# Moving the adjacency's combinations into the first graph's attention of a two-layer graph network

## The chip, the core and the metric

The kernel runs on one core of a Trainium2 chip. The metric is the device time of one execution in microseconds (us), from the first to the last instruction. Five engines run at the same time, each through its own list of instructions in order, and meet only through semaphores: PE (matrix products and transposes), DVE (elementwise work and reductions), ACT (activations and copies), POOL (elementwise work, and it issues DMA transfers) and SP (it only issues DMA transfers). An instruction that has to wait holds up everything behind it on its engine.

## The reference, cut to what matters

There are B = 16 graphs of N = 1024 nodes with C = 256 features, all with the same adjacency matrix.

```
# layer 0, for each graph
h  = relu(layernorm(x))
A_s = 2 * | |sigmoid(mean_j - mean_i) - 0.5| - 0.5 |      # weights of pairs of nodes
g  = relu((h^T @ (adj * A_s)) * para)                     # para: 256 x 1024
q  = g^T; k, v = h @ kv_w
x  = x + softmax(q k^T * scale) v                         # 4 heads of 64
# layer 1
h  = relu(layernorm(x))
An = adj + I
deg = columnsums(An) + rowsums(An) - diagonal(An)
A_hat = An * rsqrt(deg)[:, None] * rsqrt(deg)[None, :]
x  = x + batchnorm(relu(batchnorm((A_hat @ h) @ W1^T + b1)) @ W2^T + b2)
```

The batch norms are taken over all graphs. Two things in layer 1 are independent of the graph and are made once: the degrees, and sums and differences of blocks of `An` for a block matrix product with seven instead of eight products (the "combinations").

## The kernel before, in words

**The main loop.** `attention()` walks over the units of all graphs: a graph has four units (pair of heads x half of the query nodes), a unit four steps. A step issues scores (PE, 128x1024 to PSUM, L841), their exponentials (ACT, L849), the running sum of the exponentials (DVE, L868 and L871), and the product with the values for the step before (PE, L882). At a unit's end `sums()` makes the row sums (PE, L899), copies them to a tile `row` (ACT, L901), and POOL sends them through DRAM (`sums_d<-row`, L902, then `inv<-sums_d`, L907). Two steps later `add_output()` uses `inv` on DVE.

**The background.** Beside the attention of graph b, `background(b)` yields pieces of other work, each with an estimated cost; `attention()` takes pieces until a due amount is reached in each step (`advance`). `weave(main, (start, side), ...)` walks through `main` and takes one piece of each side from `main`'s piece number `start` on. `soon(action)` puts an action behind the next piece. The order in which the code emits instructions is the order on each engine: nothing is rearranged later.

Beside graph b stand the keys, values and queries of graph b + 1 (`keys_values`, `queries`), its weights (`weigh`: rows of the adjacency, Abs and Tanh on ACT, L401 and L409, a product with the row on DVE, L388), and layer 1's first product and hidden layer for graph b - 1 (`aggregate`, `hidden`). Graphs 0 and 1 get their queries by `plain_queries`, sixteen pieces that PE works through two per step; graphs from 2 on by `queries`, with seven products. The last of these is `seventh`: it adds the product and by `soon` lets `finish(1, 0)` follow, which multiplies a block of q by `para` on DVE (L449). Then come the values: four pieces of a matmul `pv` (PE) and two copies out of PSUM (DVE, L591), in one of two PSUM banks in turn.

**The degrees** (`degrees()`) run beside graph 0, woven in from its first pieces on: for each of eight 128-row tiles of the transposed adjacency a load (SP, L204), a copy with accumulated sum (ACT, L220), and two small operations for the diagonal (DVE, L222, L223); at the end a reciprocal root on POOL (`rsqrt`, L81 and L82). `columns_of(dinv)` then spreads the result on DVE (`cb_deg`, L188), and PE transposes it to `cbp_deg` (L199), from where ACT copies it to `dbc` (L200).

**The combinations** (`graph()`) run beside graph 1 in eight pieces, two per 256-row pair of blocks. A piece loads 128x1024 twice by SP (`au_f`, L239), adds the identity where the diagonal lies (POOL, L246), makes four differences (POOL, L251 to L254), and stores seven blocks to DRAM by three transfers from POOL (`aht_d`, L256 to L258). `aggregate` reads `aht_d` later, beside graph 1 for the first time.

**Buffers.** The pieces' `au_f` tiles, the rows of `weigh` and the tiles of `degrees` share the three buffers "adj". The pieces' `two` and `one`, the tiles `row`, `cb_deg`, `cb_c` and `y` share the four buffers "y", handed out in turn: who takes one waits until its last user, four takings before, is done. `w1` (weights of the hidden layer) and `dbc` have a place each, first needed beside graph 1.

Of the kernel before, what the change touches and what calls it, by code (L numbers as in the profile page):

```python
# [10 lines left out]
F32 = mybir.dt.float32  # L11
# [6 lines left out]
P = 128  # L18
# [5 lines left out]
def gnn_two_layers_kernel(  # L24
# [12 lines left out]
    nc = tc.nc  # L37
# [8 lines left out]
    TH = 2  # L46
# [37 lines left out]
    def layers(shifted):  # L84
# [30 lines left out]
        def soon(action):  # L115

            queue.append(action)
# [87 lines left out]
            return tile_  # L205

        deg_sm = big.tile([P, 6, NT], F32, name="deg")
        w1 = big.tile([P, CC, H1], F32, name="w1")
        dbc = const.tile([P, N], F32, tag="dbc", name=f"dbc_{kind}")
        row, diag, col, deg, tmp_deg, dinv = (deg_sm[:, i, :] for i in range(6))  # L210

        def degrees():

            nc.sync.dma_start(out=w1, in_=w1_t.rearrange("(k p) j -> p k j", p=P))
            nc.vector.tensor_reduce(row, rows.rearrange("p q t -> p t q"), AX.X, ALU.add)
            for t in range(NT):
                a = load_adj_t(t, "at")
                yield 0.0
                blk = a[:, t * P : (t + 1) * P]
                nc.scalar.activation(a, a, AF.Copy, accum_out=col[:, t : t + 1])  # L220
                db = p1.tile([P, P], F32, tag="s1", name=f"db_{t}")
                nc.vector.tensor_mul(db, blk, ident)  # L222
                nc.vector.tensor_reduce(diag[:, t : t + 1], db, AX.X, ALU.add)  # L223
                yield 0.0
            nc.vector.tensor_add(deg, col, row)
            nc.vector.tensor_sub(deg, deg, diag)
            rsqrt(dinv, deg, 1.0, tmp_deg)

        def graph():


            HT, HB = NT // 2, FB // 2
            for t in range(HT):
                for part in range(2):
                    cols = slice(part * HB, (part + 1) * HB)
                    a = p3.tile([P, 2, NH, HB], F32, tag="adj", name=f"au_{kind}_{t}_{part}")
                    for n in range(2):
                        r = slice((t + n * HT) * P, (t + n * HT + 1) * P)
                        nc.sync.dma_start(  # L239
                            out=a[:, n], in_=adj_t[r].rearrange("p (m c) -> p m c", m=NH)[:, :, cols]  # L240
                        )
                    yield 0.0
                    for n in range(2):
                        if part == t * P // HB:
                            blk = a[:, n, n, t * P % HB : t * P % HB + P]
                            nc.gpsimd.tensor_add(blk, blk, ident)  # L246
                    two = py.tile([P, 2, HB], F32, tag="y", name=f"two_{t}_{part}")
                    one = py.tile([P, HB], F32, tag="y", name=f"one_{t}_{part}")
                    b12, b21, b22 = a[:, 0, 1], a[:, 1, 0], a[:, 1, 1]
                    sub = nc.gpsimd.tensor_sub  # L250
                    sub(two[:, 0], b12, a[:, 0, 0])  # L251
                    sub(two[:, 1], b22, two[:, 0])
                    sub(b12, b22, b12)
                    sub(one, b21, two[:, 1])  # L254
                    dst = aht_d[:, t // TH, :, t % TH, cols].rearrange("i p c -> p i c")
                    nc.gpsimd.dma_start(out=dst[:, :4], in_=a.rearrange("p n m c -> p (n m) c"))  # L256
                    nc.gpsimd.dma_start(out=dst[:, 4:6], in_=two)
                    nc.gpsimd.dma_start(out=dst[:, 6], in_=one)  # L258
                    yield 0.0

        class Norm:

# [166 lines left out]
        def queries(b):  # L429
# [65 lines left out]

            def seventh(m):
                add(c21, m, c21)
                soon(lambda: finish(1, 0))

            for i, (left, right, midway, after) in enumerate(  # L500
                (
# [94 lines left out]
        def aggregate(b):  # L596


            pieces = []
            order = (0, 2, 5, 1, 4, 6, 3)  # L600

            def load(upto):
                while len(pieces) <= min(upto, 7 * NP // 2 - 1):
                    i, th = divmod(len(pieces), NP // 2)
                    i = order[i]
                    a = p8.tile([P, TH, FB], F32, tag="w", name=f"aht_{b}_{i}_{th}")
                    nc.sync.dma_start(out=a, in_=aht_d[i, th])
                    pieces.append(a)

            load(4)  # L610
            yield 0.0
            a11, a12, a21, a22 = quarters("b", b)
            at = ats[b] = [
                p3.tile([P, CC, FB], F32, tag="ht", name=f"at_{b}_{g}") for g in range(NH)
            ]
            c11, c12, c21, c22 = (at[g][:, c, :] for c in (0, 1) for g in (0, 1))
            add, sub = nc.vector.tensor_add, nc.vector.tensor_sub

            def scale(c, g):
                nc.vector.tensor_mul(c, c, dbc[:, g * FB : (g + 1) * FB])  # L620

            def first(m):
                nc.scalar.copy(c12, m)
                sub(a11, s1s["b", b], a11)

            def second(m):
                add(c11, m, c12)
                sub(a12, a12, a11)
                soon(lambda: scale(c11, 0))

            def fifth(m):
                add(c22, m, c21)
                add(c12, m, c12)
                soon(lambda: scale(c22, 1))

            def sixth(m):
                add(c21, m, c21)
                soon(lambda: scale(c21, 0))

            def seventh(m):  # L640
                add(c12, m, c12)
                scale(c12, 1)

            for i, (left, after) in enumerate(
                (
                    (a11, first),
                    (a12, second),
                    (a11, lambda m: add(c12, m, c12)),
                    (a21, lambda m: add(c21, m, c12)),
                    (None, fifth),  # L650
                    (a22, sixth),
                    (a12, seventh),
                )
            ):
                made = bank(f"pa_{b}_{i}")
                left = left or s1s["b", b]
                for th in range(NP // 2):
                    n = i * NP // 2 + th
                    load(n + 5)
                    for j in range(TH):  # L660
                        t = th * TH + j
                        product(
                            made, left[:, t, :], pieces[n][:, j, :], t == 0, t == NT // 2 - 1
                        )
                    if th == NP // 2 - 1:
                        after(made)
                    elif i == 0:
                        combine("b", b, nc.vector)
                    yield 1.71

        def hidden(b):
# [7 lines left out]
            for n, (g, j) in enumerate(parts):  # L679
                i = b * NH + g  # L680
                made = bank(f"py_{i}_{j}")
                for k in range(CC):
                    product(
                        made, w1[:, k, j * P : (j + 1) * P], at[g][:, k, :], k == 0, k == CC - 1
                    )
                y = py.tile([P, FB], F32, tag="y", name=f"y_{i}_{j}")
                nc.scalar.activation(y, made, AF.Identity, bias=b1[:, j : j + 1])  # L687
# [47 lines left out]
        def background(b):  # L735

            if b == 0:
# [8 lines left out]
                w, products = weighers[1], keys_values(1)  # L746
# [12 lines left out]
                broadcast_row(dbc, cbs, "deg")  # L759
                yield 1.0  # L760
                yield from prepare(2, products)
                return
# [1 line left out]
            gather = aggregate(b - 1)  # L764
            if b + 1 < B:
                w, products, norm = weighers[b + 1], keys_values(b + 1), normed(b - 1)
                combined = graph() if b == 1 else iter(())
                yield from weave(islice(products, 4), (0, islice(w, 4)), (0, islice(combined, 4)))
                yield from weave(
                    queries(b + 1), (0, double(w)), (0, combined), (9, islice(norm, 5))  # L770
                )
                yield next(gather)
                yield from weave(products, (0, norm))
            else:
# [218 lines left out]
        with st:  # L993
            if shifted:
                for b in range(B):
# [6 lines left out]
                    run(islice(weighers[b], AHEAD))  # L1002
                    run(weave(plain_queries(b), (0, weighers[b])))
                    if b == 0:
                        run(degrees())
                        broadcast_row(dbc, columns_of(dinv, "deg"), "deg")
# [5 lines left out]
                    if b == 0:  # L1012
                        run(graph())
# [355 lines left out]
```

## Time and profile before

| | before |
|---|---|
| time, median of 3 runs | 2678.98 us (2678.57 to 2681.39) |
| span of the profiled execution | 2678.6 us |
| mean granted PE clock | 0.986 |
| busy DVE | 1744.0 us |
| busy ACT | 1336.8 us |
| busy POOL | 552.8 us |
| DMA, mean over the span | 133 GB/s |
| one 128x1024 operation: p<-sc on ACT, acc<-acc,p on DVE | 1019 ns, 1224 ns |
| one 64x512 matmul, pg<-w,h_a | 594 ns (they overlap: 24 take 5.32 us) |

How to read it: busy time on its engine is a line's mean duration times its count. What decides is which engine never rests, and for the stretches where it does, what ended its pause. In the timeline a pause stands in brackets at a row's end, with the operation that ended it: `[0.79 <-DVE v L591]`. A row of the waits has the waiting operation, what it waited for, and then the sum in us, the number of times and the longest. A row of a table by stretch has the stretch, its length in us, then the busy us (and instructions) of PE, of PE's weight loads, of DVE, ACT and POOL, then the granted clock, the share of the DMA engines and GB/s.

### The profile page before, as it was taken

What the parts mean: (1) busy time and instruction counts of PE and PEld (TensorE: products, weight loads), DVE (VectorE), ACT (ScalarE), POOL (GpSimd) and SP (SyncE); (2) the same over time, 40 slices, a digit from 0 to 9 for tenths busy, and PEclk for the clock granted to TensorE, in tenths of its full rate; (3) what the DMA queues carried; (4) which work ended last, traced back from release to release, by engine and by line L of the source; (5) the groups of instructions that cost most, each with busy time, mean ns of one, the idle gap of its engine ahead of it and who ended that gap; (6) DMA issues with size and microseconds to landing.
All of it is one profiled execution on the core that took longest, in us unless ns stands there. A gap on an engine that the chain in (4) does not pass through costs nothing. (4 is left out here: it accounts for less than half of the span.)

```text
span 2678.6 us, 32187 instructions
## 1 busy us (share of the span) xinstructions
PE 2577.6 (96%) x11882; PEld 953.2 (36%) x11882; DVE 1744.0 (65%) x2768; ACT 1336.8 (50%) x1937; POOL 552.8 (21%) x632
## 2 busy tenths in 40 slices
PE   8897899999999999999999999999999999999994
PEld 3232333333333333333333333333333333334443
DVE  5556576666767575766667676757676675557674
ACT  5652363735455454636364544545463633335544
POOL 1016111111111111111111111111112111126653
PEclk9999899999999999999999999999999999999997
DMA  4325524242333414242524233242424233455559
GB/s 165 105 66 182 183 83 170 79 152 88 130 103 95 134 61 172 79 169 83 170 79 142 91 124 113 75 152 66 169 83 169 79 117 104 133 198 199 193 181 369
DMA packets 134759, 355.60 MB, mean 133 GB/s; under 512 B 17984, under 2 KB 38976, under 8 KB 128448
## 3 DMA queue, kind: packets, MB, share of 16 engines
q1 hardware_dynamic: 109120, 278.44, 30.3%
q0 software_dynamic: 25472, 75.00, 8.4%
q8 instruction: 96, 1.57, 0.2%
q14 instruction: 71, 0.58, 0.1%
HBM read 278.67 MB, written 74.71 MB: 132 GB/s over the span
## 5 line engine op out<-in xcount | busy, mean ns | idle before, releaser
L849 ACT ACTIVATE p<-sc 128x1024 f32<-128x1024 f32 x512 | 495.3, 1019 | 615.8 <-PE sc L841 615.1
L871 DVE TENSOR_TENSOR acc<-acc,p 128x1024 f32<-128x1024 f32 x384 | 470.1, 1224 | 143.6 <-ACT p L849 123.3
L841 PE MATMUL sc<-q,k 64*128 64x512 f32 x2048 | 512.7, 619 | 11.3 <-ACT p L849 11.3
L882 PE MATMUL o<-p,v 128*64 128x512 f32 x2048 | 496.4, 605 | 0.0
L158 PE MATMUL pg<-w,h_a 128*64 128x512 f32 x1600 | 359.7, 594 | 10.1 <-DVE w L388 4.9
L158 PE MATMUL pa<-aht,h_b 128*64 128x512 f32 x1536 | 343.5, 592 | 0.0
L841 PEld LDWEIGHTS sc<-q,k 64*128 64x128 f32 x2048 | 177.1, 187 | 333.8 <-issue 291.7
L902 POOL DMA_DIRECT2D sums_d<-row x64 | 37.6, 588 | 1053.8 <-ACT row L901 1053.8
L158 PE MATMUL py<-at,w 128*64 128x512 f32 x1024 | 230.4, 592 | 0.0
L388 DVE SCALAR_TENSOR_TENSOR w<-w,adj 128x1024 f32<-128x1024 f32 x128 | 157.1, 1227 | 108.2 <-ACT w L409 97.3
L882 PEld LDWEIGHTS o<-p,v 128*64 128x64 f32 x2048 | 124.4, 136 | 285.8 <-issue 283.7
L158 PEld LDWEIGHTS pg<-w,h_a 128*64 128x64 f32 x1600 | 115.4, 137 | 239.5 <-issue 211.3
L158 PEld LDWEIGHTS pa<-aht,h_b 128*64 128x64 f32 x1536 | 110.3, 137 | 213.3 <-issue 198.1
L687 ACT ACTIVATE y<-py,vec 128x512 f32<-128x512 f32 x128 | 87.6, 684 | 168.4 <-PE py L158 111.4
L401 ACT ACTIVATE w<-cbc,csum 128x512 f32<-128x512 f32 x256 | 170.0, 715 | 0.0
L868 DVE TENSOR_TENSOR acc<-p,p 128x1024 f32<-128x1024 f32 x64 | 78.9, 1233 | 109.3 <-ACT p L849 109.3
L158 PE MATMUL pv<-kvw_f,ht 128*64 128x256 f32 x1024 | 122.8, 388 | 24.1 <-DVE v L591 15.7
L409 ACT ACTIVATE w<-w 128x1024 f32<-128x1024 f32 x128 | 135.0, 1054 | 1.8
L688 POOL DMA_DIRECT2D y_d<-y x128 | 70.0, 547 | 316.3 <-ACT y L687 309.1
L463 DVE TENSOR_TENSOR w<-w,w 128x1024 f32<-128x1024 f32 x112 | 134.4, 1230 | 1.5
L907 POOL DMA_DIRECT2D inv<-sums_d x128 | 98.2, 771 | 136.1 <-DMA sums_d<-row 96.0
L158 PEld LDWEIGHTS py<-at,w 128*64 128x64 f32 x1024 | 74.2, 137 | 145.2 <-issue 128.4
(154 smaller groups left out, 2854.7 us busy)
## 6 DMA issues: line engine op xcount, KB each, us to landing
aht<-aht_d SPq DMA_DIRECT2D x224, 512.0 KB, 6.0
adj<-in_adj_dram SPq DMA_DIRECT2D x128, 512.0 KB, 4.3
y_d<-y POOLq DMA_DIRECT2D x128, 256.0 KB, 2.7
yin_f<-y_d SPq DMA_DIRECT2D x32, 1024.0 KB, 6.4
x<-in_x_dram SPq DMA_DIRECT2D x32, 512.0 KB, 5.1
para<-in_para_dram SPq DMA_DIRECT2D x64, 256.0 KB, 3.9
x_d<-x POOLq DMA_DIRECT2D x16, 1024.0 KB, 10.2
xo_f<-x_d SPq DMA_DIRECT2D x32, 512.0 KB, 8.8
```

Source lines behind the costliest of these rows:

```text
L158: nc.tensor.matmul(dst[r], left[:, r], right, start=start, stop=stop)
L388: nc.vector.scalar_tensor_tensor(w, w, 1.0, a, op0=ALU.add, op1=ALU.mult)
L401: nc.scalar.activation(w[:, t, :], cbc[:, q * FB : (q + 1) * FB], AF.Abs, bias=csum[:, th * TH + t : th * TH + t + 1], scale=-1.0,)
L409: nc.scalar.activation(made[i], made[i], AF.Tanh, scale=-0.5 / C)
L463: nc.vector.tensor_sub(block(i)[part], block(x)[part], block(y)[part])
L687: nc.scalar.activation(y, made, AF.Identity, bias=b1[:, j : j + 1])
L841: nc.tensor.matmul(sc[:, e, :], ks[b][k][r, m * P : (m + 1) * P], qs[b][k][r, f * FB : (f + 1) * FB], start=True, stop=True,)
L849: nc.scalar.activation(pr, sc, AF.Exp)
L868: nc.vector.tensor_add(self.acc, self.held, pr)
L871: nc.vector.tensor_add(self.acc, self.acc, pr)
L882: nc.tensor.matmul(self.o[r, :], vs[b][k][:, m, r], pr[:, e, :], start=(m == 0), stop=(m == NT - 1),)
L907: nc.gpsimd.dma_start(out=self.inv[:, :, e], in_=sums_d[u][e].rearrange("(j q) -> q j", q=P))
```

## The change

The eight pieces of combinations move from graph 1's background to graph 0's. They no longer use the "adj" buffers: a piece is loaded to the place of `w1` or of `dbc` by turns, which stand empty until then, and the load is issued by POOL, one piece ahead, between a piece's second and third difference. `w1` is loaded, and `dbc` made, only after that (`load_later`). The column sums start later (from `plain_queries`' eighth piece, where they began with the keys) and are loaded two tiles ahead. And `finish(1, 0)` after `seventh` comes two pieces later instead of one. The amount of work does not change. It is meant to take the pieces and their loads out of the way of graph 1's rows, and the column sums out of a stretch in which ACT is busy.

```diff
         def degrees():
-            nc.sync.dma_start(out=w1, in_=w1_t.rearrange("(k p) j -> p k j", p=P))
             nc.vector.tensor_reduce(row, rows.rearrange("p q t -> p t q"), AX.X, ALU.add)
+            ahead = [load_adj_t(t, "at") for t in range(2)]
+            yield 0.0
             for t in range(NT):
-                a = load_adj_t(t, "at")
-                yield 0.0
+                a = ahead[t]
...
+                if t + 2 < NT:
+                    ahead.append(load_adj_t(t + 2, "at"))
                 yield 0.0
...
         def graph():
-                    a = p3.tile([P, 2, NH, HB], F32, tag="adj", name=f"au_{kind}_{t}_{part}")
-                        nc.sync.dma_start(
+            def load():
+                u = len(loaded)
+                t, part = divmod(u, 2)
+                pool, tag = ((big, "w1"), (const, "dbc"))[part]
+                a = pool.tile([P, 2, NH, HB], F32, tag=tag, name=f"au_{kind}_{u}")
+                for n in range(2):
+                    nc.gpsimd.dma_start(
...
+            load()
+            yield 0.0
+            for u in range(2 * HT):
...
+                sub(two[:, 0], b12, a[:, 0, 0])
+                sub(two[:, 1], b22, two[:, 0])
+                if u + 1 < 2 * HT:
+                    load()
+                sub(b12, b22, b12)
+                sub(one, b21, two[:, 1])
...
+        def load_later():
+            later["w1"] = big.tile([P, CC, H1], F32, tag="w1", name="w1")
+            nc.sync.dma_start(out=later["w1"], in_=w1_t.rearrange("(k p) j -> p k j", p=P))
+            later["dbc"] = const.tile([P, N], F32, tag="dbc", name=f"dbc_{kind}")
...
             def seventh(m):
                 add(c21, m, c21)
-                soon(lambda: finish(1, 0))
+                soon(lambda: soon(lambda: finish(1, 0)))
...
-                norm, sums = Norm(2, True).all(), degrees()
                 yield from weave(
-                    islice(products, 4),
-                    (0, double(islice(w, 8))),
-                    (0, islice(sums, 4)),
-                    (0, islice(norm, 4)),
+                    islice(products, 4), (0, double(islice(w, 8))), (0, islice(norm, 4))
                 )
-                yield from weave(plain_queries(1), (0, w), (0, sums), (0, norm))
+                yield from weave(
+                    plain_queries(1), (0, norm), (0, w), (5, graph()), (7, degrees())
+                )
+                load_later()
                 yield from islice(products, 1)
                 cbs = columns_of(dinv, "deg")
...
-                combined = graph() if b == 1 else iter(())
-                yield from weave(islice(products, 4), (0, islice(w, 4)), (0, islice(combined, 4)))
+                yield from weave(islice(products, 4), (0, islice(w, 4)))
```

A second copy of the kernel, for inputs whose exponentials leave the range of the numbers, is changed in the same way; it is not executed for these inputs.

More of the change, by code (lines that the diff above doesn't have):

```diff
@@ L207, in layers @@
         deg_sm = big.tile([P, 6, NT], F32, name="deg")
-        w1 = big.tile([P, CC, H1], F32, name="w1")
-        dbc = const.tile([P, N], F32, tag="dbc", name=f"dbc_{kind}")
+        later = {}
         row, diag, col, deg, tmp_deg, dinv = (deg_sm[:, i, :] for i in range(6))
         def degrees():
-            nc.sync.dma_start(out=w1, in_=w1_t.rearrange("(k p) j -> p k j", p=P))
             nc.vector.tensor_reduce(row, rows.rearrange("p q t -> p t q"), AX.X, ALU.add)
+            ahead = [load_adj_t(t, "at") for t in range(2)]
+            yield 0.0
             for t in range(NT):
-                a = load_adj_t(t, "at")
-                yield 0.0
+                a = ahead[t]
                 blk = a[:, t * P : (t + 1) * P]
@@ L232, in graph @@
             HT, HB = NT // 2, FB // 2
-            for t in range(HT):
-                for part in range(2):
-                    cols = slice(part * HB, (part + 1) * HB)
-                    a = p3.tile([P, 2, NH, HB], F32, tag="adj", name=f"au_{kind}_{t}_{part}")
[L237 to L259, printed above, removed]
@@ new lines, in graph @@
+            loaded = []
+            def load():
+                u = len(loaded)
+                t, part = divmod(u, 2)
+                cols = slice(part * HB, (part + 1) * HB)
+                pool, tag = ((big, "w1"), (const, "dbc"))[part]
+                a = pool.tile([P, 2, NH, HB], F32, tag=tag, name=f"au_{kind}_{u}")
+                for n in range(2):
+                    r = slice((t + n * HT) * P, (t + n * HT + 1) * P)
+                    nc.gpsimd.dma_start(
+                        out=a[:, n], in_=adj_t[r].rearrange("p (m c) -> p m c", m=NH)[:, :, cols]
+                    )
+                loaded.append(a)
@@ new lines, in graph @@
+            load()
+            yield 0.0
+            for u in range(2 * HT):
+                t, part = divmod(u, 2)
+                cols = slice(part * HB, (part + 1) * HB)
+                a = loaded[u]
+                for n in range(2):
+                    if part == t * P // HB:
+                        blk = a[:, n, n, t * P % HB : t * P % HB + P]
+                        nc.gpsimd.tensor_add(blk, blk, ident)
+                two = py.tile([P, 2, HB], F32, tag="y", name=f"two_{u}")
+                one = py.tile([P, HB], F32, tag="y", name=f"one_{u}")
+                b12, b21, b22 = a[:, 0, 1], a[:, 1, 0], a[:, 1, 1]
+                sub = nc.gpsimd.tensor_sub
+                sub(two[:, 0], b12, a[:, 0, 0])
[4 more added lines that the diff above has]
+                sub(one, b21, two[:, 1])
+                dst = aht_d[:, t // TH, :, t % TH, cols].rearrange("i p c -> p i c")
+                nc.gpsimd.dma_start(out=dst[:, :4], in_=a.rearrange("p n m c -> p (n m) c"))
+                nc.gpsimd.dma_start(out=dst[:, 4:6], in_=two)
+                nc.gpsimd.dma_start(out=dst[:, 6], in_=one)
+                yield 0.0
@@ L619, in scale @@
             def scale(c, g):
-                nc.vector.tensor_mul(c, c, dbc[:, g * FB : (g + 1) * FB])
+                nc.vector.tensor_mul(c, c, later["dbc"][:, g * FB : (g + 1) * FB])
             def first(m):
@@ L683, in hidden @@
                     product(
-                        made, w1[:, k, j * P : (j + 1) * P], at[g][:, k, :], k == 0, k == CC - 1
+                        made, later["w1"][:, k, j * P : (j + 1) * P], at[g][:, k, :], k == 0, k == CC - 1
                     )
@@ L745, in background @@
                     yield 1.0
-                w, products = weighers[1], keys_values(1)
-                norm, sums = Norm(2, True).all(), degrees()
+                w, products, norm = weighers[1], keys_values(1), Norm(2, True).all()
                 yield from weave(
-                    islice(products, 4),
-                    (0, double(islice(w, 8))),
-                    (0, islice(sums, 4)),
-                    (0, islice(norm, 4)),
-                )
-                yield from weave(plain_queries(1), (0, w), (0, sums), (0, norm))
+                    islice(products, 4), (0, double(islice(w, 8))), (0, islice(norm, 4))
+                )
+                yield from weave(
+                    plain_queries(1), (0, norm), (0, w), (5, graph()), (7, degrees())
+                )
+                load_later()
                 yield from islice(products, 1)
@@ L758, in background @@
                 yield TOP
-                broadcast_row(dbc, cbs, "deg")
+                broadcast_row(later["dbc"], cbs, "deg")
                 yield 1.0
@@ L766, in background @@
                 w, products, norm = weighers[b + 1], keys_values(b + 1), normed(b - 1)
-                combined = graph() if b == 1 else iter(())
-                yield from weave(islice(products, 4), (0, islice(w, 4)), (0, islice(combined, 4)))
-                yield from weave(
-                    queries(b + 1), (0, double(w)), (0, combined), (9, islice(norm, 5))
-                )
+                yield from weave(islice(products, 4), (0, islice(w, 4)))
+                yield from weave(queries(b + 1), (0, double(w)), (9, islice(norm, 5)))
                 yield next(gather)
@@ L1004, in layers @@
                     if b == 0:
-                        run(degrees())
-                        broadcast_row(dbc, columns_of(dinv, "deg"), "deg")
+                        run(degrees(), graph())
+                        load_later()
+                        broadcast_row(later["dbc"], columns_of(dinv, "deg"), "deg")
                     run(keys_values(b))
@@ L1011, in layers @@
                     nc.gpsimd.dma_start(out=x1_d[b], in_=xs[b])
-                    if b == 0:
-                        run(graph())
                     if b == B - 1:
```

## The prediction

> **What bounds the kernel now.** I read the page first. PE is busy 96% of the span, DVE 65%, ACT 50%, so a change helps only where it removes a pause of PE, and hurts where it makes one.
>
> ```profile
> PE 2577.6 (96%) x11882; PEld 953.2 (36%) x11882; DVE 1744.0 (65%) x2768; ACT 1336.8 (50%) x1937; POOL 552.8 (21%) x632
> PE   8897899999999999999999999999999999999994
> ```
>
> The slices say that the pauses lie in the first tenth. Next, the busy time by stretch, cut where a graph's last row sums leave POOL (192.96, 368.23, 514.06, 659.91 us): graph 1's attention, then graphs 2 and 3.
>
> ```profile
> 192.96:368.23 175.27, 153.26 (x698) 54.32 (x696) 104.68 (x156) 74.05 (x109) 71.89 (x94) 0.92 0.48 162
> 368.23:514.06 145.83, 145.04 (x698) 51.88 (x696) 98.26 (x156) 74.12 (x109) 22.41 (x30) 1.00 0.35 116
> 514.06:659.91 145.85, 145.05 (x698) 51.88 (x696) 98.27 (x156) 74.11 (x109) 22.42 (x30) 1.00 0.35 116
> ```
>
> The same 698 PE instructions take 175.3 us in graph 1 and 145.85 later: **graph 1 loses 29.4 us**. It alone has the adjacency's pieces, 49 us more of POOL. PE's timeline there shows where:
>
> ```profile
> 227.75 3.21 PE L158 MATMUL pg<-w,h_a 128*64 128x512 f32 x8 [4.89 <-DVE w L388]
> 253.02 3.78 PE L841 MATMUL sc<-q,k 64*128 64x512 f32 x8 [2.96 <-ACT p L849]
> 270.42 3.68 PE L158 MATMUL pv<-kvw_f,ht 128*64 128x256 f32 x16 [8.39 <-DVE q L497]
> 279.87 3.42 PE L158 MATMUL pv<-kvw_f,ht 128*64 128x256 f32 x16 [5.77 <-DVE v L591]
> ```
>
> The four pauses are 22.0 us, and the matmuls after them run slow (3.21 where eight take 1.89), some 7.8 us more. The waits of ACT and SP in that window name the pieces:
>
> ```profile
> ACT row L901 <- DMA aht_d<-two: 15.7, 1, 15.7
> SPq L239 <- DMA aht_d<-au_f: 38.3, 5, 9.5
> SPq L170 <- DVE w L388: 38.3, 2, 34.3
> ```
>
> ACT stands 15.7 us for a "y" buffer that a piece's store holds. SP stands 38.3 us because each piece's load needs one of three "adj" buffers that an earlier piece is being stored from, with the weighing rows and para queued behind.
>
> Graph 0 has smaller pauses, from ACT: 12.3 us in all, 11.3 between 84 and 130 us (1.89, 0.86, 5.39, 1.26, 1.26, 0.66), plus 1.6 us of slow matmuls after the long one. ACT waits there for the column sums' rows:
>
> ```profile
> ACT at L220 <- DMA at<-in_adj_t_dram: 9.3, 3, 4.0
> ```
>
> **What the Trainium skill says.** SBUF — State Buffer, section "SBUF: two separate sides": DVE and GpSimd share a port pair by an exclusive lock, and the later operation waits out the whole of the other. The trace agrees: a 128x256 subtraction on POOL takes 0.72 us when DVE rests, 1.7 beside it. TensorE: Matmul & The Clock Gate, section "What's actually happening": after an idle window of about 3.4 us PE runs at half clock until about 3.4 us busy. The trace agrees roughly: 1.5 to 2.8 us extra after a pause, even after 2.96 us of one. DMA: Bandwidth & Descriptors, section "Anatomy of one DMA": about 2.0 us and the bytes at 436e3 a us for a DMA issued by POOL. That is an estimate of 2.6 us for 256 KB; the trace's such stores take 3.7, which I use.
>
> **Part 1, the pieces leave graph 1.** All four pauses hang on them: the late rows and para (SP's queue), the held "y" buffer (ACT), the norm's small POOL operations behind subtractions (8.39: DVE waited 7.6 us for POOL's lnsm_b). Nothing else differs from graph 2, so graph 1 should take 145.85 us: **-29.4**.
>
> **Part 2, the product with para two pieces later.** In every later graph PE waits once, before the third values matmul:
>
> ```profile
> 425.68 0.69 DVE L449 TENSOR_TENSOR q<-q,para 128x512 f32<-128x512 f32 x1
> 426.28 1.41 DVE L591 COPY v<-pv 128x256 f32<-128x256 f32 x4
> 427.18 1.95 PE L158 MATMUL pv<-kvw_f,ht 128*64 128x256 f32 x16 [0.79 <-DVE v L591]
> ```
>
> The product (0.60 us from start to start) stands ahead of the copies that free the bank. In the changed order it comes after the first two copies, so PE waits 0.79 - 0.60 = 0.19. The next bank is needed only after scores and output matmuls (3.9 us), so nothing is passed on. Fourteen graphs do this: 14 x 0.6 = **-8.4**. Its consumer, the next graph's second half, is over 50 us away.
>
> **Part 3, the pieces and the late sums in graph 0.** Column sums leave ACT's busy part: PE's 11.3 + 1.6 = 12.9 us there go. In the place where they stand now (after 120 us) ACT waits for PE, so they cost nothing. But POOL now has a chain in front of the reciprocal root of the degrees. That root (L82) stands behind all eight pieces in POOL's order; cb_deg on DVE waits for it, the transposes cbp_deg on PE for cb_deg. Before, there were 21 us between:
>
> ```profile
> 145.38 1.67 POOL L82 TENSOR_TENSOR deg<-deg,neg_half 128x8 f32<-128x8 f32 x1
> 166.19 0.75 DVE L188 COPY cb_deg<-deg 128x512 f32<-128x512 f32 x2
> 169.90 1.09 PE L199 MATMUL cbp_deg<-ident,cb_deg 128*128 128x128 f32 x8
> ```
>
> When does POOL get there?
> - Start: the first piece's load stands behind the first unit's inv, issued until 111.2. Its row came late because ACT held three column sums (3 x 1.25) and waits for them (1.38 + 3.99), 9.1 us; so 102.1. First half 0.7, then second half's landing 3.5 (as au_f's before, its median): first piece at 106.3.
> - One piece: four subtractions, 4.85 us on average in the first four pieces of before (DVE busy), 2.9 in the fastest; diagonal 0.5 on average (8 x 0.45 over 8); three stores 0.78 + 0.71 + 0.57 = 2.06; the next load now on POOL too, two issues, priced like the 256 KB store at 0.71: 1.42. So 8.8 beside DVE, 6.9 with DVE at rest. A store lands 3.5 us after issue and a load too, both inside the piece, so no wait is added.
> - Five pieces at 8.5 to 8.8, about 43; two at 6.9 and the last, without a load, at 5.5 (DVE by then stands at cb_deg): 19.3. The second unit's sums among them: 0.57 + 1.87 waiting + 1.51, 3.9. Root 0.25 + 1.67, 1.9. Two microseconds for landings that come late (they reach 5.5). Sum 70; the root is done at **176**.
>
> PE, without its old pauses, reaches cbp_deg at 169.9 - 12.9 = 157, and stands until 176.5: some 19.5 us, with ACT (next unit's row, waiting for the seventh piece's store in "y") and DVE standing too. Add 1.8 us of half clock. The time at this point moves by 176.5 + 1.8 - 169.9 = **+8.4**. Behind it nothing else gets late: w1's load waits for the seventh piece's store, and the third unit's inv lands some 6.6 us after the root, PE needs it 7 after.
>
> Bounds of the unknown, one piece: 7 us (root at 106.3 + 56 - 1.4 + 3.9 + 1.9 = 167, so -1) to 10 us (191, so +23).
>
> Sum: -29.4 - 8.4 + 8.4 = -29.4, so 2679.0 - 29.4 = 2649.6, say **2650**.
>
> **The rivals.**
> - A, POOL is no obstacle: the root is done by 156 us, for which a piece may take (156 - 106.3 - 5.8 + 1.4)/8 = 5.7 us. Then graph 0 gains 12.9 as well: -50.7, **2628**. For it: pieces of 4.9 to 5.7 us exist in the trace. Against: without loads, and beside a resting DVE.
> - B, POOL is slower: every subtraction at 1.71 (6.8), diagonal 0.5, stores 2.06, load 1.42, some late landing: 11 us. Root at 106.3 + 88 - 1.4 + 5.8 = 199; +31; sum -7, **2672**. For it: DVE is denser once PE's pauses go. Against: DVE stops by itself at cb_deg.
> - C, slower: as B, and graph 1 keeps half its loss because rows and para are late for another reason: -14.7 - 8.4 + 31 = +8, **2687**. Against: graph 2 has the same rows and para without a pause.
>
> **How the numbers follow.** Main case 0.58, A 0.15, B 0.15, C 0.08, the rest something unseen. With a piece from 7 to 10 us the main case spans 2640 to 2664; taking in most of A and part of B, the range is 2630 to 2668. 0.2% is 5.4 us, so faster means under 2673.6: main, A, over half of B: 0.85; same 0.06 (rest of B); slower 0.09.
>
> **What would show it.** Right: the stretch of graph 1 near 146 us with PE at 145; no pause at its third values matmul beyond 0.2 us; in graph 0 one pause of 12 to 25 us at cbp_deg, released by cb_deg, and cb_deg by POOL's root at 167 to 185; column sums with no pause of PE about them. Wrong: the root done before 157 (A); pieces of 11 us (B); a pause of several us left in graph 1 (C), or a new one in graph 0 ahead of cbp_deg, where ACT's row for the second unit waits for a store in "y".

## The result, and the profile after

The changed kernel takes **2660.45 us** (median of 4 runs, 2659.76 to 2661.65) against 2680.18 us (2678.57 to 2682.12) for the kernel before beside it: ratio 0.9927, interval 0.9909 to 0.9944, so 19.7 us less. The prediction was 2650 with a range of 2630 to 2668. The profiled span is 2658.7 us against 2678.6.

The page of the changed kernel, busy time and PE's slices:

```profile
PE 2572.0 (97%) x11882; PEld 951.8 (36%) x11882; DVE 1743.4 (66%) x2768; ACT 1336.5 (50%) x1937; POOL 564.0 (21%) x648
PE   8959999999999999999999999999999999999995
```

The work is the same. Slices 2, 4 and 5, which were 8, 7 and 8 tenths, are 9 now; but the third slice (133 to 199 us) fell from 9 to 5, a hole that wasn't there. The busy time by stretch, cut where a graph's last row sums leave POOL as for the kernel before (211.63, 356.88, 501.98 us), is

```profile
211.63:356.88 145.25, 145.06 (x698) 51.89 (x696) 98.28 (x156) 74.12 (x109) 22.43 (x30) 1.00 0.35 117
356.88:501.98 145.10, 144.90 (x698) 51.82 (x696) 98.26 (x156) 74.12 (x109) 22.41 (x29) 1.00 0.34 117
```

Graph 1 went from 175.27 to 145.25 us, graph 2 from 145.83 to 145.10. So the difference of the spans comes in three: graph 0 ends 211.63 - 192.96 = +18.7 later, graph 1 is 30.0 shorter, and all that follows takes 2301.8 us instead of 2310.4, 8.6 shorter. 18.7 - 30.0 - 8.6 = -19.9, which is the difference of the spans. **Graph 1 and the later graphs did what was forecast; graph 0 lost 18.7 where 8.4 was reckoned.** From 60 us to graph 0's end PE's timeline has these pauses of over 3 us, and no others:

```profile
153.10 3.57 PE L158 MATMUL pv<-kvw_f,ht 128*64 128x256 f32 x16 [5.16 <-DVE q L575]
182.93 1.12 PE L199 MATMUL cbp_deg<-ident,cb_deg 128*128 128x128 f32 x4 [17.98 <-DVE cb_deg L188]
187.68 1.09 PE L199 MATMUL cbp_deg<-ident,cb_deg 128*128 128x128 f32 x4 [3.63 <-DVE v L612]
```

The waits of the first graph's stretch, with the sum, the number and the longest in us, tell who waited ahead of PE:

```profile
ACT row L918 <- DMA aht_d<-two: 22.4, 2, 15.7
DVE cb_deg L188 <- POOL deg L82: 21.4, 1, 21.4
POOL inv L924 <- DMA sums_d<-row: 12.7, 3, 7.3
DVE cb_deg L188 <- DMA aht_d<-two: 3.6, 1, 3.6
ACT at L219 <- DMA at<-in_adj_t_dram: 2.9, 3, 1.1
```

The last row was 9.3 us before: the column sums' rows no longer come late. The first two are new doors: both "y" buffers and the root stand behind POOL's pieces. POOL's own timeline, about the second unit's sums and at the end of the chain, and DVE's behind the former:

```profile
134.98 0.57 POOL L919 DMA_DIRECT2D sums_d<-row  x1
142.86 1.56 POOL L924 DMA_DIRECT2D inv<-sums_d  x2 [7.30 <-DMA sums_d<-row]
...
180.74 1.67 POOL L82 TENSOR_TENSOR deg<-deg,neg_half 128x8 f32<-128x8 f32 x1
```

```profile
146.31 0.20 DVE L942 RECIPROCAL inv<-inv 128x8 f32<-128x8 f32 x1 [7.57 <-DMA inv<-sums_d]
```

POOL stood 7.30 us in the middle of its chain for a transfer of 4 KB, and the root came at 180.74 + 1.67 = 182.4. Even PE's 5.16 us pause at 153 hangs on it: `inv` could be issued only at 142.86, DVE waited 7.6 us for it with its reciprocal, and the query products (`q<-pg,para`) that free PE's banks stood behind that.

### The profile page after: what moved, and what is told of

Its sections match the earlier page's. It is cut to its first block, busy times and chain, and to the rows that moved or that the text cites. A ratio compares the mean times of both kernels' runs of the same rounds, so it can differ in the third digit from the quotient of the medians.

```text
span 2658.7 us, 32181 instructions
## 1 busy us (share of the span) xinstructions
PE 2572.0 (97%) x11882; PEld 951.8 (36%) x11882; DVE 1743.4 (66%) x2768; ACT 1336.5 (50%) x1937; POOL 564.0 (21%) x648
## 3 DMA queue, kind: packets, MB, share of 16 engines
q1 hardware_dynamic: 104768, 274.25, 29.4%
## 6 DMA issues: line engine op xcount, KB each, us to landing
x_d<-x POOLq DMA_DIRECT2D x16, 1024.0 KB, 10.3
```

## The experiments

Under each, "less" is the median against that of the kernel before beside it (2679.71, 2677.76, 2680.59 or 2677.94 us). "Changed" is the kernel after the change (19.7 less). Only the intervals of runs 1, 9, 10 and 11 are clear of that of changed (0.9909 to 0.9944); smaller differences from it are what the medians say, and not certain.

**1. The last product alone.** The kernel before, with this edit only:

```diff
-                soon(lambda: finish(1, 0))
+                soon(lambda: soon(lambda: finish(1, 0)))
```

> The kernel before with the last product with para two pieces later and nothing else. Theory (the product stands ahead of the copies that free a PSUM bank): fourteen graphs gain 0.6 us each, 8.4 us, ratio 0.9969; the pause of PE at the third values matmul falls from 0.79 to 0.19 us. Rival (the product only moves in front of other copies that PE needs as soon): no change, ratio 1.000.

Measured 2671.46 us, ratio 0.9969 (0.9957 to 0.9982), 8.2 less. DVE's and PE's timelines in graph 2:

```profile
423.06 0.75 DVE L591 COPY v<-pv 128x256 f32<-128x256 f32 x2
423.73 0.68 DVE L449 TENSOR_TENSOR q<-q,para 128x512 f32<-128x512 f32 x1
424.33 0.74 DVE L591 COPY v<-pv 128x256 f32<-128x256 f32 x2
...
423.96 1.95 PE L158 MATMUL pv<-kvw_f,ht 128*64 128x256 f32 x16 [0.19 <-DVE v L591]
```

The product now stands between the copies, and PE's 0.79 us pause is 0.19, as the theory has it. One moved DVE operation of 0.6 us, 14 times over, is two fifths of what the whole change brought.

**2. The consumer of the root out of the way.** Changed, with the degrees' columns and `w1`'s load beside graph 1, after its first four products:

```diff
-                load_later()
-                yield from islice(products, 1)
-                cbs = columns_of(dinv, "deg")
...
+                if b == 1:
+                    load_later()
+                    cbs = columns_of(dinv, "deg")
+                    yield TOP
+                    broadcast_row(later["dbc"], cbs, "deg")
```

> The changed kernel with the spreading of the degrees (cb_deg, its transposes, dbc) and the load of w1 moved from graph 0 to graph 1, behind the keys. Theory (POOL's backlog stops graph 0 at three doors: cb_deg behind the root, ACT's row behind a piece's store, inv behind the root on POOL): only the first door opens, ACT's row still waits until about 177 and inv comes about 190, so 5 to 12 us of the 21.6 us pause come back: 25 to 32 us under the kernel before, ratio 0.988 to 0.9907. Rival (cb_deg's wait is the whole of it): the pause goes, 42 us under before, ratio 0.984.

Measured 2656.03 us, 0.9911 (0.9897 to 0.9924), 23.7 less: 4 us back of the 21.6 that PE stood at cbp_deg, a little under the 25 to 32 expected, and far from the rival's 42. PE's timeline, and then the waits:

```profile
154.54 3.68 PE L158 MATMUL pv<-kvw_f,ht 128*64 128x256 f32 x16 [6.25 <-DVE q L575]
180.81 3.65 PE L858 MATMUL sc<-q,k 64*128 64x512 f32 x8 [9.66 <-ACT p L866]
```

```profile
ACT row L918 <- DMA aht_d<-two: 22.4, 2, 15.6
DVE cb_c L188 <- DMA aht_d<-one: 13.2, 1, 13.2
```

The pause at cbp_deg is gone and another stands in its place, 2 us earlier: ACT's `row` waits as long as ever for a "y" buffer, and exponentials, then scores, behind it. So the root was one of several doors that opened at the same moment, when POOL got through its pieces. Nor are the columns free beside graph 1: cut at the last row sums as before (205.05 and 353.04 us), graph 0 ends 6.6 us earlier than changed, but graph 1 takes 148.0 us instead of 145.25, 1.0 for the columns' transposes and 1.7 for a new pause of PE.

**3. The column sums where they were.** Changed, with `degrees()` woven in from the keys on and one tile at a time, as before the change:

```diff
-            ahead = [load_adj_t(t, "at") for t in range(2)]
...
-                    plain_queries(1), (0, norm), (0, w), (5, graph()), (7, degrees())
+                    plain_queries(1), (0, norm), (0, w), (0, sums), (5, graph())
```

> The changed kernel with the column sums back at their old start and their old loads, one tile at a time. Theory (the end of POOL's chain sets graph 0's time): PE's small pauses of 11 us come back but are swallowed by the pause at cbp_deg; the chain starts 9 us later, its transfers have less beside them, so the root is done at 181 to 186: 16 to 22 us under the kernel before, ratio 0.992 to 0.994. Rival (the earlier sums cost PE their 12.9 us again): 7 us under before, ratio 0.9974.

Measured 2664.16 us, 0.9941 (0.9927 to 0.9955), 15.6 less, just outside the 16 to 22 expected and far from the rival's 7. The expectation's root at 181 to 186 was wrong: it stands ahead of the last two pieces and is done at 170.4, 12 us earlier than changed. Yet PE stands nearly as long at the same place:

```profile
180.18 1.11 PE L199 MATMUL cbp_deg<-ident,cb_deg 128*128 128x128 f32 x4 [9.56 <-DVE cb_deg L188]
189.57 1.08 PE L199 MATMUL cbp_deg<-ident,cb_deg 128*128 128x128 f32 x4 [8.28 <-DVE v L609]
```

```profile
DVE cb_deg L188 <- DMA aht_d<-one: 12.0, 1, 12.0
DVE cb_deg L188 <- DMA aht_d<-two: 8.2, 1, 8.2
```

Each half of `cb_deg` takes a "y" buffer and waits for a piece's store. This is the second door, without the first. It also prices the late column sums: some 4 us, not the 12.9 of old pauses, since PE gets earlier to a place where it then stands longer.

**4. One row ahead instead of two.** Changed, with the column sums' rows loaded one tile ahead (`range(1)`, `t + 1`).

> The changed kernel with the column sums' tiles loaded one ahead instead of two. Theory (the sums' row loads, two to three at a time, fill the DMA engines, so POOL's small transfer of the second unit's sums lands late, 7.9 us): it lands in about 3 us, the root is done about 5 us earlier, 24 to 26 us under the kernel before, ratio 0.990 to 0.991. Rival (the transfer waits behind POOL's own loads and stores in its queue): no change from the changed kernel, 20 us under before, ratio 0.9927.

Measured 2660.11 us, 0.9923 (0.9910 to 0.9937), the same as changed, as the rival has it. POOL still waits 6.16 us for `sums_d` (7.30 in changed). The number of rows ahead is no gain, and at most a small part of the cause.

**5. The pieces' loads by SP.** Changed, with

```diff
-                    nc.gpsimd.dma_start(
+                    nc.sync.dma_start(
                         out=a[:, n], in_=adj_t[r].rearrange("p (m c) -> p m c", m=NH)[:, :, cols]
```

> The changed kernel with the pieces' loads issued by SP instead of POOL. Theory (the length of POOL's chain of pieces sets graph 0's time): POOL is rid of eight pairs of issues of 1.43 us, 11 us; the root and the last stores come about 11 us earlier, 28 to 32 us under the kernel before, ratio 0.988 to 0.9896. Rival (transfers set the pace: a load waits for the store out of its place whoever issues it, and SP holds the column sums' loads behind it): no change from the changed kernel, 20 us under before, ratio 0.9927.

Measured 2651.82 us, 0.9901 (0.9886 to 0.9916), 25.9 less, between the theory's 28 to 32 and the rival's 20. POOL is relieved: the root is done at 172.7, ACT's rows wait 0.5 us in all. But SP's queue became a door, since rows of the column sums stand behind loads whose place isn't free:

```profile
ACT at L219 <- DMA at<-in_adj_t_dram: 26.8, 4, 13.8
PE sc L858 <- ACT p L866: 11.8, 3, 9.9
ACT row L918 <- DMA aht_d<-two: 0.5, 1, 0.5
```

**6. The pieces earlier.** Changed, with `(0, graph())` for `(5, graph())`: they begin five query pieces earlier.

> The changed kernel with the pieces woven in from the first piece of the queries instead of the sixth. POOL rests from about 92 to 98.6 us, so the chain starts 6 to 10 us earlier. Theory (where the chain ends sets graph 0's time): 26 to 30 us under the kernel before, ratio 0.9888 to 0.9903. Rival (pieces that early hold up POOL's small operations for the norm and the first unit's sums, and ACT and DVE with them): new pauses of PE ahead of 130 us, and 15 to 22 us under before.

Measured 2662.67 us, 0.9941 (0.9927 to 0.9954), 15.1 less, so by the medians 4 to 5 us worse than changed; the 26 to 30 of the theory are out. The time is in the rival's range, but its new pauses ahead of 130 us are not there. An earlier start of POOL's chain was no gain, because of one wait of ACT:

```profile
158.65 0.58 ACT L918 COPY row<-sums 128x512 f32<-128x512 f32 x1 [32.30 <-DMA aht_d<-two]
```

```profile
162.29 3.78 PE L858 MATMUL sc<-q,k 64*128 64x512 f32 x8 [24.15 <-ACT p L866]
```

POOL's third piece begins to be stored, then the eighth, and the second unit's sums behind it:

```profile
125.21 0.78 POOL L271 DMA_DIRECT2D aht_d<-au_f  x1
...
160.22 0.78 POOL L271 DMA_DIRECT2D aht_d<-au_f  x1
...
162.27 0.57 POOL L919 DMA_DIRECT2D sums_d<-row  x1
```

This was the run that overturned "the end of POOL's chain is the wall". The pieces are put into the program at one per query piece, and sixteen of those pass in some 65 us of PE, 4 us each; POOL needs 6 to 11 us from one piece's first store to the next. When ACT began to wait, at 126.4, POOL had just stored its third piece, while the program had handed out all eight: `sums_d` of this unit stands behind the eighth piece on POOL's queue (stored from 160.22, `sums_d` at 162.27), and the "y" buffer handed to `row` came free only after the seventh's store (from 154.48). In the changed kernel three pieces stand ahead of it.

**7 and 8. The earlier start with the late columns, and with SP's loads too.** The edit of 6 with that of 2, and then with that of 5.

> The changed kernel with the pieces from the first piece of the queries and the degrees spread in graph 1. Theory (two doors, the root's chain and the stores in the row buffers, both move 6 to 10 us earlier, and the first is no longer waited for in graph 0): PE stands less than 6 us about the third unit's start, 30 to 38 us under the kernel before, ratio 0.986 to 0.989. Rival (the two do not add, since the stores alone set the end): as the earlier start alone.

> The changed kernel with three edits: the pieces' loads by SP, the pieces from the first piece of the queries, the degrees spread in graph 1. Theory: POOL's chain ends about 20 us earlier than in the changed kernel, ahead of everything that waits for it, so graph 0 keeps no pause over 3 us there: 42 to 50 us under the kernel before, ratio 0.981 to 0.984. Rival (transfers set the pace): pauses of 10 us or more stay in graph 0, 25 to 35 us under before.

Measured 2662.48 us (0.9942, 0.9928 to 0.9955) and 2660.05 us (0.9932, 0.9919 to 0.9946), 15.3 and 17.7 less. In 7 ACT's row waits 32.4 us as in 6: the consumer of the root isn't what holds it. In 8 the row waits for nothing, but 31.6 us in all go to rows of the column sums behind the pieces' loads on SP's queue, and PE pauses 22.17. Run 7 is as its rival had it, as the earlier start alone; run 8 falls short of even its rival's 25 to 35. Three edits, two of which help alone, are together worse than the best of them alone.

**9. Pieces at POOL's pace.** The edit of 6, and one piece per two query pieces, by a `yield` more in each:

```diff
                 yield 0.0
+                yield 0.0
...
-                    plain_queries(1), (0, norm), (0, w), (5, graph()), (7, degrees())
+                    plain_queries(1), (0, norm), (0, w), (0, graph()), (7, degrees())
```

> The changed kernel, with the combinations started at the first query piece of graph 0 instead of the sixth, and one handed out per two query pieces instead of one per one; nothing else. Theory (pieces are issued at twice POOL's pace, and whoever takes a "y" buffer or follows on POOL's queue waits for the backlog): with issue in step with POOL (about 8 us a piece both) ACT's row for the second and third unit waits under 5 us each (22.4 in all and 15.7 at most in the changed kernel, 32.3 in the run that only started earlier), the root is done near 173, PE stands at cbp_deg about 12 us, 20 to 30 us under the kernel before. Rival (only the number of pieces still ahead of POOL at the end counts, and that is as large here): ACT's row again over 12 us, 15 to 20 under.

Measured 2651.16 us, 0.9886 (0.9870 to 0.9903), **29.4 less**, as expected, and with an interval clear of run 6's. The only difference from run 6 is the pace, and it is worth 14 us. PE's timeline of this kernel, and ACT's:

```profile
154.93 3.37 PE L158 MATMUL pv<-kvw_f,ht 128*64 128x256 f32 x16 [3.67 <-DVE q L576]
175.62 1.11 PE L199 MATMUL cbp_deg<-ident,cb_deg 128*128 128x128 f32 x4 [9.04 <-DVE cb_deg L188]
180.30 1.09 PE L199 MATMUL cbp_deg<-ident,cb_deg 128*128 128x128 f32 x4 [3.57 <-DVE v L613]
```

```profile
132.20 0.58 ACT L919 COPY row<-sums 128x512 f32<-128x512 f32 x1 [5.21 <-DMA aht_d<-two]
169.46 0.58 ACT L919 COPY row<-sums 128x512 f32<-128x512 f32 x1 [6.23 <-POOL two L264]
```

The 32 us wait is 5.2 and 6.2; "under 5 each" was a little too bold. The root is done at 175.1 (173 expected) and the pause at cbp_deg is half of changed's.

**10 and 11. Paced, with the columns late, and with SP's loads.** The edits of 9 and 2; then 5 as well.

> The run before, and the degrees' columns (cb_deg, cbp_deg, dbc) and w1's load moved behind the first four products of graph 1's background. Theory: with issue in step and the consumer of the root out of the way, no stall of PE over 5 us is left between 50 and 220 us; 33 to 42 us under the kernel before. Rival (POOL's work of some 8 us a piece is itself the wall, since the third unit's inv stands behind the root on its queue): a pause of PE behind inv or behind "y" of 8 us or more, about 25 under, as where only the columns were moved.

> The run before, and the pieces' loads issued by SP instead of POOL. Theory: POOL's chain is 1.4 us a piece shorter, root near 162, and with loads paced by the pieces the column sums' rows behind them on SP's queue wait under 8 us (30.1 where the loads by SP were issued early): 38 to 46 under the kernel before. Rival (SP's queue is the next door: rows of the column sums and of the weights behind a load whose place isn't free): ACT stands over 10 us at a row, 20 to 28 under.

Measured 2648.45 us (0.9880, 0.9863 to 0.9896; runs 2646.76 to 2650.58) and 2649.47 us (0.9882, 0.9866 to 0.9899), 32.1 and 31.1 less. Both miss their forecast, the first by one, the second by seven. The first is the lowest of all and beats both kernels, the changed one by 12 us, though its runs and those of 9 (2649.64 to 2653.09) overlap. ACT and PE in it:

```profile
133.61 0.59 ACT L919 COPY row<-sums 128x512 f32<-128x512 f32 x1 [7.04 <-DMA aht_d<-two]
170.87 0.58 ACT L919 COPY row<-sums 128x512 f32<-128x512 f32 x1 [10.77 <-POOL two L264]
...
172.44 3.78 PE L859 MATMUL sc<-q,k 64*128 64x512 f32 x8 [6.09 <-ACT p L867]
```

The third unit's row still waits for a piece, so a pause of 6 us remains. With SP's loads no row waits, but a column sum's row is 11.8 us late, as the rival said, and PE pauses 6.89. Either way pauses of 13.65 us are left in all between 60 and 215 us; the kernel before had 12.24 there.

**12. No rows beside the second unit's sums.** The edits of 10, and the column sums begun at the fourteenth query piece, three there and the rest beside the values and graph 2's preparation:

```diff
-                    plain_queries(1), (0, norm), (0, w), (0, graph()), (7, degrees())
+                    plain_queries(1), (0, norm), (0, w), (0, graph()), (13, islice(late, 3))
                 )
+                products = weave(products, (0, late))
```

> The run with paced pieces and late columns, and the column sums moved too: from the eighth query piece to the fourteenth, three there and the rest beside the values and the second graph's preparation, so that no row of theirs is loaded between 128 and 142 us. Question: why POOL waits 5.0 us (7.1 and 7.3 in other runs) for sums_d's landing at 137 us. Theory (their rows fill the DMA engines there, share 0.99): the wait falls to 1.7 to 3 us and the share at 136 to 140 us to under 0.6; with the root behind the third unit's inv on POOL and 10 us of ACT's work out of the busy stretch, 34 to 38 us under the kernel before (32.1 without it). Rival (the store waits for POOL's own piece transfers ahead of it): the wait stays at 4 to 7, and the time within 2 us of 32 under.

Measured 2651.97 us, 0.9903 (0.9886 to 0.9919), 26.0 less: the time missed the 34 to 38 expected, and new pauses of 2.9 and 2.1 us come at graph 2's transposes. The question it was built for, why POOL waits so long for `sums_d`, is answered only together with the other runs. Changed first, then this kernel; the columns are those of the tables by stretch, the last two the share of the DMA engines and GB/s:

```profile
136.00:140.00 4.00, 4.00 (x22) 1.48 (x20) 1.67 (x5) 2.97 (x4) 0.00 (x0) 1.00 1.00 387
```

```profile
136.00:140.00 4.00, 4.00 (x20) 1.45 (x18) 1.96 (x2) 2.23 (x4) 2.21 (x4) 1.00 0.70 238
140.00:144.00 4.00, 4.00 (x22) 1.29 (x18) 0.00 (x0) 0.79 (x2) 2.40 (x4) 1.00 0.03 5
...
141.51 1.57 POOL L927 DMA_DIRECT2D inv<-sums_d  x2 [3.30 <-DMA sums_d<-row]
```

The wait for `sums_d` is 4.97 us in run 10, and 3.30 without the rows beside it. One wait by itself says little, since runs 9 and 10 are the same program up to there and have 7.12 and 4.97. But the second unit's waits of all runs fall into groups:

- With rows loaded beside it and a piece's three stores issued just ahead on POOL's queue: 4.97 to 8.19 us (changed and runs 2, 4, 6, 7, 9, 10). Where the last store was 1.0 and 2.2 us before (runs 5 and 8): 4.82 and 4.09.
- With the stores and without rows: 3.30 here, and 2.66 in run 3, whose last rows were issued 8 us before.
- With rows and without the stores: 2.78 in run 11, where the last store was 8.3 us before. The share of the DMA engines from 136 to 140 us was 0.85 there, and 0.88 in run 9.
- With neither, in graph 0 of the kernel before: 1.87.

So, as far as these few cases go, neither makes the long wait alone, and the two together do; how full the engines are isn't enough to tell. Nor is a busy DVE enough: in changed it stood idle for the last 4 us of the wait (138.8 to 142.9), longer than the whole wait is without rows. The third unit's sums say the same: POOL waits 4.1 us where SP loads `w1` and rows beside the last piece's stores (changed and run 9), and 1.8 where it doesn't (runs 2 and 10). The Trainium skill, DMA: Bandwidth & Descriptors, section "Queues, rings and completion order", gives a way for both: each DMA engine takes turns between queues packet by packet, and the semaphore's increment lands only after every earlier write of that engine, whatever its queue. A 4 KB store would then report when what is in flight has been written. The runs agree with it and don't prove it.

## Why the prediction was right, and by how much not

Forecast -29.4 in all, measured -19.7: inside the range, and the main case, with one part sized too low.

- **Part 1, the pieces leave graph 1: right.** 29.4 forecast. Graph 1 is 30.0 shorter, of which Part 2 has 0.6. "All four pauses hang on them": none is left.
- **Part 2, 14 x 0.6: right.** 8.4 forecast, 8.2 by itself (run 1). The pause of 0.19 came out at 0.19 to 0.20 in ten graphs and at 0.55 in two.
- **Part 3, graph 0: +8.4 forecast, +18.7 measured.** The form was right: PE stood 17.98 us at cbp_deg (19.5 forecast), behind cb_deg, behind POOL's root. So was the cost of a piece, in sum: without waits the first took 10.6 us, with 2.6 of it at its diagonal, and the others, from first store to first store, 8.3, 7.4, 7.9, 7.7, 8.0, 6.5 and 5.7, where 8.5 to 8.8 (five), 6.9 (two) and 5.5 were forecast. (A piece's two loads are 256 KB each, 128x512, as the prediction priced them; the description of the kernel has them twice as large.) These steps were not right:
  - "The second unit's sums among them: 0.57 + 1.87 waiting + 1.51": the 1.87 was 7.30, 5.4 over. And "a store lands 3.5 us after issue and a load too, both inside the piece, so no wait is added", with "two microseconds for landings that come late": POOL waited 1.51 and 1.70, 1.2 over. The first piece began 0.8 earlier, and the pieces without waits took 62.2 us together, 62.3 forecast; that this fits so closely is luck, since a first piece that was too long made up for shorter ones. So the root came at 182.4, not 176 (0.4 of it was rounded off): **+6.4**. The landing times were taken from a profile in which the DMA engines were 0.40 busy between 90 and 160 us; with the pieces among them it was 0.59, and 1.00 where `sums_d` was stored.
  - cb_deg was costed as one operation. It is two, each with a "y" buffer of its own. The second waited 3.57 us for the last piece's store, issued at 179.06 and landed at about 186.4: 7.4 us where 3.5 was used. SP had issued `w1`'s load and three rows of the adjacency, 2 MB, just ahead (175.79 to 177.74), and the DMA engines were full from 178 to 186 us (0.96 to 1.02). PE's second pause, **3.6**.
  - 6.4 + 3.6 = 10.0 of the 10.3 us that were missing.
  - "PE, without its old pauses, reaches cbp_deg at 157": it came at 182.93 - 17.98 = 165, because of the 5.16 us pause at 153 and the half clock after it (3.57 us for sixteen values matmuls, 1.90 otherwise). That cost nothing, as PE then stood the less at cbp_deg. So the 12.9 us weren't gained either, as the sum had it.
- **The rivals.** A (POOL no obstacle, 2628) is out, and no run got there: the best is 18.6 us above the -50.7 of A. B (11 us a piece) is out by its mechanism, though the time lies halfway to it: pieces after the first took 6 to 8 us. C is out by graph 1.
- **The signs.** One of those for being wrong appeared in part: a new pause of PE ahead of cbp_deg, the 5.16 us at 153. ACT's row for the second unit did wait 6.7 us for a store in "y", as named there, but POOL was in a piece until after that; the pause came from `inv`, and cost nothing for the reason just given.
- **What the prediction didn't see** is that the root was only the last of several doors. Its "Behind it nothing else gets late" was about the time after; ahead, it named ACT's row as waiting but took it as free since PE stood anyway. Runs 2, 3 and 5 to 8 show that with one door open the next one holds: row, both halves of cb_deg or cb_c, `inv`, and with loads by SP the column sums' rows. Run 6 against 9 shows the cause common to those on POOL: pieces put into the program twice as fast as POOL works.

Open: how POOL's stores and SP's loads hold each other up in the DMA engines, since the runs show only that it takes both; and whether pieces with buffers of their own would take the last doors away. The latter wasn't tried, as there is no room for eight "y" buffers.

## What to carry to other kernels

Work that is moved beside other work should be put into the program at the pace of the engine that does it: one that is handed out faster puts its backlog ahead of everything that shares its buffers or its queue, and then an earlier start can be no gain, or a loss. Before moving it, list every taker of those buffers and every later instruction on that queue; removing one wait of several that end together gives back only the difference to the next. And take landing times from a stretch with the traffic that will be there, not from one with a third less (0.40 against 0.59 here), and look at what stands ahead on the same queue.

## What the hardware showed that was not expected

- `sums_d`'s 4 KB store from POOL landed 1.8 us after issue in the median of 95 to 192 us before the change; with rows loaded beside it and a piece's stores just ahead on its queue POOL waited 5.0 to 8.2 us for it, with either alone 2.7 to 3.3. The 512 KB loads for the column sums took 5.9 us in the median, 3.7 before.
- PE ran slow after every pause of over 3 us that these runs show before values matmuls, and after some of 2: sixteen of them took 3.57 us after a pause of 5.16, 3.37 after 3.67 (run 9), 3.17 after 3.01 (run 11), but also 2.98 after 2.07 (run 5, granted clock 0.60 from 164 to 166 us), against 1.95 after 2.00 (run 6). The length of the pause alone doesn't decide it at 2 us.
